# One sample's lookup table, written in front of the scan instead of beside it

## The chip, the cores and the metric

The kernel runs on one core of a Trainium2 chip and processes four images one after the other, with the stages of neighbouring images overlapped. The metric is the device time of one execution, in microseconds. The runs of the kernel before took 21982.39, 21988.68 and 22019.09 us; their median is 21988.68 us.

A core has five engines that work side by side, each through its own instructions in order: PE (TensorE) multiplies matrices, DVE (VectorE) does elementwise work and scans, ACT (ScalarE) does activations and copies, POOL (GpSimd) does elementwise work and issues the indexed gathers, SP (SyncE) issues all other DMAs. They wait for each other through semaphores.

## The reference, cut to what matters

Four layers, each of the form x + f(groupnorm(x)), on images of 128 channels and 128 x 128 pixels in float32:

```python
x = x + _L0_conv_ref(_gn(x), ...)   # deformable 3x3 convolution
x = x + _L1_conv_ref(_gn(x), ...)   # dilated 5x7 convolution and two small products
x = x + _L2_conv_ref(_gn(x), ...)   # projections, a state-space scan in 4 directions, norms
x = x + _L3_conv_ref(_gn(x), ...)   # 3x3 convolution minus a Laplacian
```

Layer 0 is what the change is about. For each pixel and each of 9 taps it samples the normalised image at a position computed from the image, by bilinear interpolation (four corners, four weights, a mask), and multiplies the samples of a tap by a 128 x 128 matrix. Layer 2 holds the heavy part: for each of 4 directions, 128 channels and 16 states a recurrence h = h * exp(delta * A) + delta * u * B over 16384 pixels.

## The kernel before, in words

An image is cut into 32 blocks of 4 rows (512 pixels). Each layer is a Python generator that emits instructions and yields its progress, a number between 0 and 1. A generator's steps are laid out by `weave` (L91): a small software pipeline in which operation `what` of block t minus its lag is emitted at step t. `store` (L133) does not emit a store at once: it puts it on a list, and `tick` (L140) counts it down, three ticks by default, and then emits it on SP.

**The table of layer 0.** `layer0_table` (L236) makes what layer 0 gathers from. It reads the image once for statistics (16 loads of 512 KB, `measure` L251 with 32 bn_stats), computes scale and shift in `gn_affine` (L210), then goes through the 32 blocks: load (256 KB, L270), normalise on ACT (L274), store the normalised block (L275), transpose on PE (four 128 x 128 transposes, L280), copy out of PSUM on ACT (L287), and four stores of 256 KB each (L290), since each entry of the table holds a pixel's four corners side by side. Eight border stores complete it. Its parameter `spare` says whether the transposes go to PSUM bank 2 (`bank(2)`) or to the two buffers `pa` that the scan uses later.

**Layer 0.** `layer0` (L300) works in 288 steps of one block and one tap. A step issues four indirect DMAs on POOL (L426), each fetching 128 table entries of 2 KB; two steps later ACT multiplies three of the corners by their weights (twelve activations, L440), DVE adds and finishes a fourth (L451, L454), PE adds and transposes into one PSUM bank (L464, L465), ACT copies out (`smp`, L469) and PE projects (L475). Every ninth step DVE adds the image (L482). The offsets for the next 16 rows (`positions`, L348) are spread over the same steps. `pw0` sits in bank 2, `pst` in bank 1, `acc` in bank 0, the offsets in bank 3.

**The order around it.** The code at L1352 to L1360 is the part in front of the scan: the first image's table is driven by hand inside the loop over `layer0(sts[0])`, three of its yields per yield of layer 0; then layer 1 of the first image runs alone, then layer 2's first part until four blocks are out. Then `together` (L1313) runs the scan of all four images as the main program, 2048 scan instructions an image (L1044), and beside it one side program. The side program is cut into one part per scanned image by `around` (L1362), and each part is a list of stages with weights that `chain` (L1281) turns into shares of the part. Side work is emitted as the scan goes on, so a stage with weight w in a list with sum W lies beside 2048 w / W scan instructions, whatever its own work is.

Beside the first image's scan the list is: the rest of layer 2's first part of image 0 (18, `begun`), the table of image 1 (12), layer 0 of image 1 (28), layer 1 (14), layer 2's first part (36); the sum is 108. Beside the second and third it is: the end of layer 2 of the image before (16), layer 3 together with the table of the image after next (34), then 28, 14, 36; the sum is 128. `loads` (L1332) marks which engine a stage keeps busy, and the scan moves some of its own work accordingly (with "POOL" some products go to DVE, with "PE" pairs are added on POOL first).

Of the kernel before, what the change touches and what calls it, by code (L numbers as in the profile page):

```python
# [10 lines left out]
F32 = mybir.dt.float32  # L11
# [7 lines left out]
P = 128  # L19
# [4 lines left out]
N = R * W  # L24
# [66 lines left out]
def weave(n, order, ready=lambda t: True):  # L91


    total = n + max(step[0] for group in order for step in group if step is not MORE)
    for t in range(total):
        while not ready(t):
            yield None
        left = iter(())
        for k, group in enumerate(order):
            for step in group:  # L100
                if step is MORE:
                    next(left, None)
                elif 0 <= t - step[0] < n:
                    more = step[1](t - step[0])
                    left = left if more is None else more
            yield (t + (k + 1) / len(order)) / total
        for _ in left:
            pass
# [3 lines left out]
def conv_preact_kernel(ctx: ExitStack, tc: tile.TileContext, a: dict, nb: int):  # L112
# [6 lines left out]
    pss = ctx.enter_context(tc.tile_pool(name="scps", bufs=1, space=PSUM))  # L119
    psb = ctx.enter_context(tc.tile_pool(name="bgps", bufs=1, space=PSUM))  # L120

    def load(pool, src, shape, name, **kw):
        t = pool.tile(shape, F32, name=name, **kw)
        nc.sync.dma_start(t, src)
        return t

    def bank(which, name):
        return psb.tile([P, N], F32, name=name, tag=f"bank{which}")
# [4 lines left out]
    def store(dst, src, after=3, of=None):  # L133

        waiting.append([after, of, dst, src])
# [4 lines left out]
    def tick():  # L140
        for w in waiting:
            w[0] -= 1
        due = [w for w in waiting if w[0] <= 0]
        waiting[:] = [w for w in waiting if w[0] > 0]
        for w in due:
            nc.sync.dma_start(*w[2:])

    def flush():
        while waiting:
            nc.sync.dma_start(*waiting.pop(0)[2:])  # L150
# [45 lines left out]
    def blk(t, i):  # L196
        return t[:, i * N : (i + 1) * N]
# [8 lines left out]
    def rsqrt(dst, src, eps):  # L206
        nc.scalar.activation(dst, src, AF.Ln, bias=eps)
        nc.scalar.activation(dst, dst, AF.Exp, scale=-0.5)

    def gn_affine(stats, which=0):  # L210

        both = bank(which, "pmv")
        mv = small.tile([P, 2], F32, name="mv")
        nc.vector.bn_aggr(mv, stats)
        pm = both[:, 0:1]
        nc.tensor.matmul(pm, gmat, mv[:, 0:1], start=True, stop=True)
        d = small.tile([P, 1], F32, name="gnd")
        nc.vector.tensor_sub(d, mv[:, 0:1], pm)
        e = small.tile([P, 1], F32, name="gne")
        nc.vector.scalar_tensor_tensor(e, d, d, mv[:, 1:2], ALU.mult, ALU.add)  # L220
        pv = both[:, 1:2]
        nc.tensor.matmul(pv, gmat, e, start=True, stop=True)
        sc = small.tile([P, 1], F32, name="gnscale")
        rsqrt(sc, pv, gn_eps)
        sh = small.tile([P, 1], F32, name="gnshift")
        nc.vector.scalar_tensor_tensor(sh, pm, -1.0, sc, ALU.mult, ALU.mult)
        return sc, sh

    def new_stats(b, layer):
        return small.tile([P, NBLK, 6], F32, name=f"stats_{b}_{layer}", tag="stats", bufs=3)  # L230

    def image(name, parts=P):
        return dram.tile([parts, HW], F32, name=name)


    def layer0_table(st, spare=True):  # L236

        xb = x_in[st["b"]].rearrange("c h w -> c (h w)")
        stats = new_stats(st["b"], 0)
        table = dram.tile([TW * TW, 4 * P], F32, name="table")  # L240
        st["rows"] = 0
        tv = table.rearrange("(y x) (q c) -> y x q c", x=TW, q=4)
        xnd = image("xnd")
        with ExitStack() as s:
            lp = s.enter_context(tc.tile_pool(name="l0l", bufs=2, side="right"))
            got = {}

            def fetch(j):
                got[j] = load(lp, xb[:, 2 * j * N : 2 * (j + 1) * N], [P, 2 * N], "xst", bufs=3)

            def measure(j):  # L251
                for i in range(2):
                    nc.vector.bn_stats(stats[:, 2 * j + i, :], blk(got[j], i))

            for f in weave(NBLK // 2, [[(0, fetch)], [(2, measure)]]):
                yield 0.25 * f
            sc, sh = gn_affine(stats, 2)
            st["table"], st["xn"] = table, xnd


            for y, q in ((0, 0), (H, 2)):
                dst = tv[y, :, q : q + 2, :].rearrange("x q c -> x (q c)")
                nc.sync.dma_start(dst[0:W], zero[0:W])
                nc.sync.dma_start(dst[W : W + 1], zero[0:1])
            for x, q, y in ((0, 0, 1), (W, 1, 1), (0, 2, 0), (W, 3, 0)):
                nc.sync.dma_start(tv[y : y + H, x, q, :], zero[:, 0:P])
            yield 0.25

            def fetch_block(i):
                got["x", i] = load(lp, blk(xb, i), [P, N], "xt", bufs=4)  # L270

            def normalise(i):
                got["n", i] = xn = lp.tile([P, N], F32, name="xn", bufs=3)
                nc.scalar.activation(xn, got["x", i], AF.Identity, bias=sh, scale=sc)  # L274
                store(blk(xnd, i), xn)  # L275

            def turn(i):
                got["t", i] = pt = bank(2, "pt") if spare else pss.tile([P, N], F32, name="pt", tag="pa", bufs=2)
                for r in range(R):
                    nc.tensor.transpose(  # L280
                        pt[:, r * P : (r + 1) * P], got["n", i][:, r * W : (r + 1) * W], ident
                    )

            def put(i):
                y = i * R
                gt = lp.tile([P, R, P], F32, name="gt", bufs=4)
                nc.scalar.copy(gt, got["t", i])  # L287
                for q in range(4):
                    ty, tx = y + 1 - q // 2, 1 - q % 2
                    store(  # L290
                        tv[ty : ty + R, tx : tx + W, q, :].rearrange("y x c -> x y c"), gt
                    )
                st["rows"] = i + 1

            for f in weave(NBLK, [[(4, put)], [(0, fetch_block), (2, normalise)], [(3, turn)]]):
                yield 0.25 + 0.75 * f
            flush()
        st["rows"] = NBLK + 1
# [982 lines left out]
    def chain(parts):  # L1281

        total = sum(w for _, w in parts)
        done = 0.0
        for stage, w in parts:
            for f in stage:
                yield None if f is None else (done + w * f) / total
            done += w
# [12 lines left out]
    def rest(stage, when):  # L1301

        first = 0.0
        while not when():
            first = next(stage)
            tick()
        return ((f - first) / (1.0 - first) for f in stage)

    def drain(gen):
        for _ in gen:  # L1310
            tick()
# [17 lines left out]
    sts = [{"b": b} for b in range(nb)]  # L1329
    last = nb - 1  # L1330

    def loads(engine, stage, spare=False):  # L1332
        for f in stage:
            beside["busy"], beside["spare"] = engine, spare
            yield f
        beside["busy"], beside["spare"] = None, False

    def head(b):
        st = sts[b]
        table = [(loads(None, layer0_table(st), True), 12)] if b < 2 else []  # L1340
        return table + [(loads("POOL", layer0(st)), 28), (loads("PE", layer1(st), True), 14),
                (loads("PE", layer2_pre(st), True), 36)]

    def tail(b):
# [5 lines left out]
        return [(post, 16), (loads(load, abreast(conv, layer0_table(sts[b + 2])), True), 34)]  # L1350

    first = head(0)  # L1352
    ahead = layer0_table(sts[0], False)
    for f in layer0(sts[0]):
        tick()
        for _ in range(3):
            next(ahead, None)
            tick()
    drain(chain(first[2:-1]))
    begun = rest(first[-1][0], lambda: sts[0].get("out", 0) >= 4)  # L1360

    def around(b):  # L1362

        side = [(begun, 18)] if b == 0 else tail(b - 1)
        if b < last:
            return side + head(b + 1)
        load, rounds = sum(w for _, w in side), NBLK + 10
        side = [(stage, (NDIR * NBLK + LATE - rounds) * w / load) for stage, w in side]
        return side + [(loads(None, layer2_post(sts[b]), True), rounds)]
# [89 lines left out]
```

## Time and profile before

| what | value |
|---|---|
| median of three runs | 21988.68 us |
| the profiled execution, its time | 22048.69 us |
| its span (first to last instruction) | 22046.9 us |
| mean granted TensorE clock | 0.913 |
| busy share PE, DVE, ACT, POOL | 80, 81, 74, 80% |
| in front of the scan (to its first instruction) | 2328.5 us |
| beside it: scans of image 0, 1, 2, 3 | 5133.9, 5207.0, 5212.5, 3828.7 us |

The profiled execution is 60.0 us longer than the median of the runs; durations below are from it. Inside the part in front of the scan the last block of image 0's table is copied out at 203.4 us, layer 0's gathers run from 220.6 to 1975.7 us, layer 1 follows, and the first scan instruction starts at 2328.5 us. The table of image 1 lies between 3050.8 and 3491.6 us, beside the first scan.

A group's line in the profile reads: line of the code, engine, operation, output and inputs by the program's names, shapes, count, then busy time in us, mean ns of one, and the idle time of the engine just before, with what ended it. A window's line reads: the window in us, its length, each engine's busy time in it with the number of instructions, the granted TensorE clock, the share of the 16 DMA engines in use, and GB/s.

### The profile page before, as it was taken

Reading aid. Unit: us, or ns where it says so; the run is one execution under the profiler, and the core shown is the slowest. Engines: PE = TensorE matmul, PEld = TensorE weight load, DVE = VectorE, ACT = ScalarE, POOL = GpSimd, SP = SyncE. Lnnn points to the kernel's source line nnn. Section 1 sums busy time; section 2 is a strip of 40 time slices with the busy share of each in tenths; the row PEclk is TensorE's granted clock in tenths of the full one; section 3 lists DMA queues with packets and bytes.
Section 4 is the critical chain, followed back from the end, with each engine's and each line's share of the span. In section 5 each row is a group of like instructions: output and inputs, shape, how many; then the busy total and the mean of one; then the engine's idle time right before and its main releaser. Section 6 shows DMA issues by size and latency. Waiting matters only on the chain. (4 is left out here: it accounts for less than half of the span.)

```text
span 22046.9 us, 206313 instructions
## 1 busy us (share of the span) xinstructions
PE 17530.0 (80%) x51536; PEld 8506.2 (39%) x51536; DVE 17759.7 (81%) x18759; ACT 16420.1 (74%) x37439; POOL 17657.2 (80%) x11985
## 2 busy tenths in 40 slices
PE   4667777888878888788888887887887878778788
PEld 3444333445323333454533333344543333233333
DVE  2332688888998899888798889978889888999984
ACT  4775777888778776788868876688877877666673
POOL 3663787667899999777789999977779999999994
PEclk7888998999989999999999999999999999999999
DMA  7666678777766878777776697777776677556674
GB/s 226 189 187 185 191 241 274 245 242 246 255 207 221 237 242 266 243 246 243 246 249 216 219 262 240 257 245 240 250 252 219 221 224 228 200 202 209 214 233 134
DMA packets 2578940, 5040.76 MB, mean 229 GB/s; under 512 B 1060736, under 2 KB 1333576, under 8 KB 2435408
## 3 DMA queue, kind: packets, MB, share of 16 engines
q1 hardware_dynamic: 2209104, 3819.31, 53.2%
q0 software_dynamic: 368640, 1208.25, 18.1%
q8 instruction: 415, 6.80, 0.1%
q14 instruction: 781, 6.40, 0.1%
HBM read 4082.03 MB, written 874.52 MB: 225 GB/s over the span
## 5 line engine op out<-in xcount | busy, mean ns | idle before, releaser
L1044 DVE TENSOR_TENSOR_SCAN h<-pa,carry,h 128x512 f32<-128x512 f32 x8192 | 10011.3, 1267 | 605.7 <-ACT pa L919 386.4
L933 PE MATMUL yacc<-h,gather_sb 128*128 128x512 f32 x15264 | 7958.5, 648 | 1906.5 <-POOL h L959 1303.9
L959 POOL TENSOR_TENSOR h<-h,cb 128x1024 f32<-128x1024 f32 x3651 | 8589.1, 2365 | 622.3 <-ACT carry L953 575.2
L426 POOL DMA_INDIRECT g<-table,idx x4608 | 4535.8, 984 | 2470.2 <-issue 1174.3
L919 ACT ACTIVATE pa<-spread,neg_a 128x512 f32<-128x512 f32 x8192 | 5488.6, 682 | 109.9 <-DVE h L1044 82.3
L933 PEld LDWEIGHTS yacc<-h,gather_sb 128*128 128x128 f32 x15264 | 2967.8, 206 | 6073.5 <-issue 2925.7
L996 DVE TENSOR_TENSOR h<-dub,bb 128x2048 f32<-128x2048 f32 (+1 forms) x2048 | 4210.4, 2056 | 519.8 <-ACT dub L893 517.4
L464 PE MATMUL pst<-ident,g 128*128 128x128 f32 x9216 | 2134.8, 319 | 1327.6 <-ACT smp L469 1097.8
L440 ACT ACTIVATE g<-g,wt 128x128 f32<-128x128 f32 x9216 | 2839.4, 390 | 42.1 <-DMA g<-table,idx 38.9
L953 ACT COPY carry<-h 128x2 f32<-128x2 f32 x4096 | 769.5, 188 | 2705.7 <-DVE h L1044 2699.4
L464 PEld LDWEIGHTS pst<-ident,g 128*128 128x128 f32 x9216 | 1686.8, 224 | 2174.2 <-ACT smp L469 1614.3
L465 PE MATMUL pst<-ident,v 128*128 128x128 f32 x9216 | 2129.5, 318 | 321.9 <-DVE v L454 170.8
L451 DVE TENSOR_TENSOR pw<-pw,g 128x512 f32<-128x512 f32 x1152 | 797.0, 692 | 1961.2 <-ACT pw L440 1555.4
L465 PEld LDWEIGHTS pst<-ident,v 128*128 128x128 f32 x9216 | 1674.8, 227 | 419.2 <-DVE v L454 225.0
L440 ACT ACTIVATE pw<-g,wt 128x128 f32<-128x128 f32 x4608 | 1691.8, 367 | 131.7 <-DVE v L454 11.4
L893 ACT COPY dub<-spread 128x512 f32<-128x512 f32 x2048 | 1195.7, 584 | 302.4 <-DVE h L996 111.8
L454 DVE SCALAR_TENSOR_TENSOR v<-g,wt,pw 128x128 f32<-128x128 f32 x4608 | 1293.6, 343 | 114.4 <-issue 2.3
L475 PE MATMUL acc<-smp,w_sb 128*128 128x512 f32 x2304 | 1287.6, 642 | 21.4 <-DVE x L482 14.8
L469 ACT COPY smp<-pst 128x512 f32<-128x512 f32 x1152 | 668.1, 580 | 776.3 <-remote 578.2
L1264 PE MATMUL p<-xn,w_l_sb 128*128 128x508 f32 (+2 forms) x2304 | 1129.7, 608 | 1.8 <-ACT xn L1243 1.8
L899 POOL TENSOR_TENSOR h<-spread,bb 128x512 f32<-128x512 f32 x845 | 1079.5, 1278 | 15.9 <-DMA spread<-stepsd 10.2
L872 POOL TENSOR_TENSOR e<-e,one_e 128x512 f32<-128x512 f32 x423 | 538.2, 1272 | 486.8 <-ACT one_e L856 463.7
(183 smaller groups left out, 18935.7 us busy)
## 6 DMA issues: line engine op xcount, KB each, us to landing
spread<-stepsd SPq DMA_DIRECT2D x2048, 512.0 KB
bb<-bcd SPq DMA_DIRECT2D x512, 1024.0 KB
cb<-bcd SPq DMA_DIRECT2D x512, 1024.0 KB
stepsd<-steps SPq DMA_DIRECT2D x512, 512.0 KB
table<-gt SPq DMA_DIRECT2D x512, 256.0 KB
g<-table,idx POOLq DMA_INDIRECT x4608
u<-urow SPq DMA_DIRECT2D x256, 256.0 KB
yrow<-y SPq DMA_DIRECT2D x256, 256.0 KB
```

The lines of the kernel that those rows point to most:

```text
L426: nc.gpsimd.indirect_dma_start(out=g[:, r].rearrange("p q c -> p (q c)"), out_offset=None, in_=table, in_offset=bass.IndirectOffsetOnAxis( ...
L440: nc.scalar.activation(pw[:, r * P : (r + 1) * P] if c == 0 else g[:, r, c, :], g[:, r, c, :], AF.Copy, scale=wv[:, r, q, k, c : c + 1],)
L454: nc.vector.scalar_tensor_tensor(v[:, r, :], g[:, r, 3, :], wv[:, r, q, k, 3:4], pw[:, r, :], ALU.mult, ALU.add)
L464: nc.tensor.matmul(dst, g[:, r, 2, :], ident, start=True, stop=False)
L465: nc.tensor.matmul(dst, v[:, r, :], ident, start=False, stop=True)
L475: nc.tensor.matmul(got["a", i], w0[:, k, :], got.pop(("c", n)), start=k == 0, stop=k == KK - 1)
L893: nc.scalar.copy(p, blocks[t]["p", g][:, 1, :])
L919: nc.scalar.activation(pa, blocks[t]["p", g][:, 0, :], AF.Exp, scale=neg_a[:, k, n : n + 1])
L933: nc.tensor.matmul(c["y"], gather[:, g, :], c["h", g][:, ng, :], start=g == 0 and ng == 0, stop=last and ng == parts[-1] and not second,)
L959: engine.tensor_mul(h, h, c["cb"][:, 2 * half : 2 * half + 2, :])
L996: nc.vector.tensor_tensor(h[:, 0:n, :], c["pdu", g].unsqueeze(1).to_broadcast([P, n, N]), c["bb"][:, 0:n, :], ALU.mult)
L1044: nc.vector.tensor_tensor_scan(o, f, o, carry[:, n : n + 1], ALU.mult, ALU.add)
```

## The change

The second image's table is taken off the list beside the first scan and is driven by hand in front of the scan, inside the loop over the first image's layer 0. It starts when layer 0 has passed 0.05 of its progress and is kept level with it from there. It writes its transposes to `pa`, and `gn_affine` takes `pa` too, since bank 2 is in use. `first` has no table entry any more, so layer 1 of image 0 is now its element 1. The countdown of stores changes with it: once the first table is finished, a yield of layer 0 ticks once, and once more for each yield of the second table, where it ticked four times before.

```diff
     def gn_affine(stats, which=0):
-        both = bank(which, "pmv")
+        both = pss.tile([P, N], F32, name="pmv", tag="pa", bufs=2) if which is None else bank(which, "pmv")
...
-            sc, sh = gn_affine(stats, 2)
+            sc, sh = gn_affine(stats, 2 if spare else None)
...
     def head(b):
         st = sts[b]
-        table = [(loads(None, layer0_table(st), True), 12)] if b < 2 else []
-        return table + [(loads("POOL", layer0(st)), 28), (loads("PE", layer1(st), True), 14),
+        return [(loads("POOL", layer0(st)), 28), (loads("PE", layer1(st), True), 14),
                 (loads("PE", layer2_pre(st), True), 36)]
...
     first = head(0)
-    ahead = layer0_table(sts[0], False)
+
+    ahead, second = (layer0_table(st, False) for st in (sts * 2)[:2])
+    at = 0.05
     for f in layer0(sts[0]):
         tick()
         for _ in range(3):
-            next(ahead, None)
+            if next(ahead, None) is not None:
+                tick()
+        while nb > 1 and f is not None and at < f:
+            at = next(second, 1.0)
             tick()
-    drain(chain(first[2:-1]))
+    if nb > 1:
+        drain(second)
+    drain(chain(first[1:-1]))
     begun = rest(first[-1][0], lambda: sts[0].get("out", 0) >= 4)
```

## The prediction

> **What bounds the kernel now.** I read the page's slices first, then the windows of each stage, then the count of scan instructions in the same windows, then the groups of layer 0 in front of the scan. In the slices, columns are busy tenths in 40 equal parts of 551 us.
>
> ```profile
> DVE  2332688888998899888798889978889888999984
> ...
> PEclk7888998999989999999999999999999999999999
> DMA  7666678777766878777776697777776677556674
> ```
>
> The first four parts, in front of the scan, leave DVE at 2 to 3 tenths, the other engines not full either, and PE at a lower clock. From then on DVE is at 8 to 9. The two regimes are limited differently, so I price them apart. The windows below are: layer 0 in front of the scan; beside the first scan `begun`, table, layer 0, layer 1, layer 2's first part; and beside the second scan layer 0, layer 1, layer 2's first part. The limits of a window are where the scan's count passes 2048 times the weight's share.
>
> ```profile
> core 0: us, PE busy (x) PEld busy (x) DVE busy (x) ACT busy (x) POOL busy (x), PEclk, DMA share, GB/s
> 220.60:1975.70 1755.10, 1168.50 (x5662) 840.68 (x5662) 626.54 (x1720) 1229.09 (x3733) 1092.78 (x1152) 0.80 0.64 187
> 2328.50:3050.80 722.30, 605.22 (x1280) 250.80 (x1280) 605.58 (x440) 606.24 (x1128) 638.12 (x364) 0.93 0.68 210
> 3050.80:3491.60 440.80, 297.96 (x640) 118.98 (x640) 407.15 (x323) 292.95 (x583) 368.57 (x199) 0.88 0.93 308
> 3491.60:5613.10 2121.50, 1716.86 (x7270) 1029.07 (x7271) 1797.36 (x2604) 1828.89 (x4990) 1438.51 (x1292) 0.92 0.74 242
> 5613.10:6118.80 505.70, 434.51 (x945) 175.54 (x943) 488.38 (x396) 352.38 (x691) 469.14 (x264) 0.96 0.78 259
> 6118.80:7462.40 1343.60, 1077.23 (x2220) 436.31 (x2220) 1189.19 (x890) 1058.04 (x2014) 1265.14 (x721) 0.92 0.66 215
> 9054.50:11065.20 2010.70, 1629.19 (x7045) 990.76 (x7044) 1598.13 (x2468) 1730.98 (x4795) 1394.10 (x1271) 0.91 0.74 241
> 11065.20:11505.40 440.20, 391.72 (x868) 160.34 (x868) 425.12 (x351) 308.78 (x603) 393.41 (x219) 0.97 0.81 268
> 11505.40:12669.40 1164.00, 960.10 (x1998) 394.75 (x1998) 1011.45 (x756) 940.74 (x1775) 1074.23 (x613) 0.92 0.66 216
> ```
>
> In the table's window DVE is busy 407.15 of 440.80 us: the scan sets the pace there, and the table costs the scan little. Beside layer 0 no engine is over 87%, ACT is first. In front of the scan ACT has 70%, PE 67%, POOL 62%, DVE 36%. The scans of two windows show what a stage carries:
>
> ```profile
> 3050.80:3491.60 440.80, 276.49 (x228) 0.88 0.93 308
> 3491.60:5613.10 2121.50, 671.79 (x533) 0.92 0.74 242
> ```
>
> Layer 0 in front of the scan, 400 to 1800 us:
>
> ```profile
> L426 POOL DMA_INDIRECT g<-table,idx x918 | 870.7, 949 | 528.7 <-ACT smp L469 252.1 <-issue 244.5 <-PE pst L465 25.5
> ...
> L469 ACT COPY smp<-pst 128x512 f32<-128x512 f32 x228 | 133.1, 584 | 391.1 <-remote 350.6 <-PE acc L475 32.3 <-PE pst L465 5.9
> ```
>
> A step takes 6.1 us (1755.1 / 288). ACT idles 391.1 us in this window in front of one instruction, the copy out of `pst`; PE waits in turn for that copy. In the timeline steps of 4.4 us, in which ACT has no gap, alternate with steps of 7.8 us, in which it waits over 3 us. So the loop is a ring PE, ACT, PE with free time in every engine. Last, what a table costs by itself, from 0 to 205 us:
>
> ```profile
> L280 PE MATMUL pt<-ident,xn 128*128 128x128 f32 x128 | 32.5, 403 | 81.4 <-ACT xn L274 81.4
> L274 ACT ACTIVATE xn<-xt,gnshift,gnscale 128x512 f32<-128x512 f32 x32 | 26.0, 813 | 92.4 <-DMA xt<-in_x_dram 92.2 <-DVE gnshift L226 0.2
> L280 PEld LDWEIGHTS pt<-ident,xn 128*128 128x128 f32 x128 | 21.0, 200 | 100.1 <-ACT xn L274 93.2 <-ACT gt L287 3.5 <-issue 3.4
> L253 DVE BATCH_NORM_STATS2 stats<-xst 128x6 f32<-128x512 f32 x32 | 20.4, 684 | 11.0 <-DMA xst<-in_x_dram 10.8
> L287 ACT COPY gt<-pt 128x512 f32<-128x512 f32 x32 | 18.2, 570 | 23.0 <-PE pt L280 21.3 <-DMA table<-gt 1.7
> ```
>
> **What the Trainium skill says.** "Perfetto Trace Analysis", section Optimization Strategy, says that a kernel with several regimes can gain when they are interleaved; the slices show the two regimes, and the change moves work between them. "TensorE: Matmul & The Clock Gate", section What's actually happening, says that the matmul clock is throttled by default and that activity releases it. The trace agrees in direction: 0.80 in layer 0 alone, 0.91 to 0.97 beside a scan. So a few transposes more should not lower it. "DMA: Bandwidth & Descriptors", section Issuing engines are not separate DMA queues, says that DMAs of all engines interleave on the same 16 DMA engines. The trace agrees: between 220 and 1975 us the gathers' queue has 59.3% of them and SP's 4.1%, which is the 0.64 of the window. SP's table traffic will therefore meet the gathers.
>
> **The change, part by part.**
>
> *Removed beside the first scan.* The stage of weight 12 goes: 440.8 us with 2048 x 12/108 = 227.6 scans. The scans do not go. With a sum of 96 instead of 108 they spread over the four stages left: `begun` 341.3 to 384.0 (+42.7), layer 0 531.0 to 597.3 (+66.4), layer 1 265.5 to 298.7 (+33.2), layer 2's first part 682.7 to 768.0 (+85.3). What another scan costs there is read from the same stages beside the second scan, which carry fewer:
> - layer 0: (2121.5 - 2010.7) / (531.0 - 448) = 1.335 us a scan, so +88.6 us
> - layer 1: (505.7 - 440.2) / (265.5 - 224) = 1.58, so +52.4 us
> - layer 2's first part: (1343.6 - 1164.0) / (682.7 - 576) = 1.683, so +143.6 us
> - `begun` has no second window; it is the same work as the stage before, so 1.683, +71.8 us
>
> Sum +356.4 us, net gain 440.8 - 356.4 = 84 us. The gain is the difference between 1.94 us a scan beside the table and 1.57 elsewhere, where scans fill holes. What cuts it: the slope should rise as DVE fills. A bare scan costs DVE 1267 ns (L1044) and a quarter of 2056 ns (L996), 1.781 us; at that price everywhere the scans cost 405 us and the gain is 36 us. At 1.5 throughout it is 99 us. I take the measured slopes. One more wait is in this range: layer 0's buffers now follow directly on layer 2's, on the same side of SBUF, so SP's weight loads wait for the release with the scan's spreads queued behind them; beside the second scan layer 0 also follows a stage on that side, so I add nothing.
>
> *Added in front of the scan.* By instruction:
> - ACT: 32 x (813 + 570) ns = 44 us. In a 4.4 us step this lengthens the ring, in a 7.8 us step it falls into ACT's wait, if it is not queued behind the waiting copy. The copy of the offsets (`pos_c`, L372, 0.6 us, once per strip) shows both: its steps are about 0.5 us longer, and the next two recover about half. Half: 22 us; bounds 0 and 44.
> - PE: 128 transposes, 32.5 us. The nine steps a strip that carry the offsets' convolution (L369, 721 ns each, 432 in the window) take 6.1 us on the mean, like the rest. So a quarter, 8 us; bounds 0 and 33.
> - DVE: 20.4 us of bn_stats beside 64% idle, and one scale-and-shift chain with PE waiting in its middle: 5 us with the last block's tail; bounds 2 and 15.
> - DMA and SP: 216 issues (16 loads of 512 KB, 32 loads, 32 stores and 128 table stores of 256 KB, 8 borders), 59 MB. SP's issue time is some 0.65 us each, 140 us, on a queue that waited 1013.8 us of 400 to 1800 for `x1` (L482). Loads are asked two table steps ahead (some 73 us), the residual for layer 0 over ten of its steps ahead: waiting behind an `x1` store hides. The changed countdown moves stores by three yields, under one step: nothing. In the DMA packets a gather lands 3.65 us after its issue (median), and ACT takes it 4.5 us later (median; 3.1 in the worst twentieth). A block's traffic comes in one burst of four stores, 1 MB, 3.6 us at the 283 GB/s of the first 205 us; delayed by at most that, the gathers are still in time: 1 us in all. Without this cover it is 32 x 2.7 us, as in the second rival.
> - POOL issues nothing new; PSUM `pa` is free until the scan.
>
> Sum 22 + 8 + 5 + 1 = 36 us, with bounds of about 3 and 93 short of the second rival.
>
> *Total.* -84 + 36 = -48 us against the profiled execution's 22048.7, that is 22000.7 for it. The median of the runs is 60.0 us lower: 21988.7 - 48 = 21941 us. Later scans are emitted as before, and nothing is late in place of the table: layer 0 of image 1 starts some 370 us earlier in the first scan, and runs longer.
>
> **The rivals.**
> 1. *No change: the scan is the bound that remains.* The slopes rise to DVE's own 1.78 us, the gain is 36 us and the front costs 36: 21989 us. For it: DVE has 92 to 97% beside table, layer 1 and second layer 1. Against it: beside layer 0 and layer 2 it has 85 to 89%, and two thirds of the moved scans go there, where ACT was busiest.
> 2. *Slower: the bursts break the ring of layer 0.* At each of 32 blocks the stores take half of the DMA engines for 5.4 us (1.5 MB with load and normalised store, at 283 GB/s), the gathers land 2.7 us late after their slack is used up, and ACT and PE pay in full: 32 x 2.7 + 44 + 33 = 163 us, total -84 + 163 = +79, 22068 us. It decides from 84 / 32 = 2.6 us a block. For it: beside the scan, with DMA at 0.74, a twentieth of the gathers land after 6.2 us or more. Against it: the slack above, and 36% of the DMA engines idle.
> 3. *The change does not do what it says.* The emitted order has the table's normalises and copies one block to about seven or eight of layer 0's steps, the last before layer 1's first; so only a wait that stretches it past layer 0 would do this: 21989 us.
>
> **How the numbers follow.** No change means within 0.2%, 44 us, about what a measurement of this kernel can tell. Forecast 0.55 (its own range 21895 to 21975; 0.47 faster, 0.08 within), first rival 0.29 (0.03 faster, 0.24 within, 0.02 slower), second 0.13 (slower), third 0.03 (within). Faster 0.50, within 0.35, slower 0.15. The range 21880 to 22025 has the forecast with the upper gain of 99 us and the low cost, and the first rival with a costlier front; it leaves the second rival out.
>
> **What would show it.** Layer 0 in front of the scan: 1755 becomes about 1791 us, no DMA wait of hundreds of us in front of L440 or L451. First scan: 5134 becomes about 5050 us, its layer 0 about 2210, layer 1 about 558, layer 2's first part about 1487, `begun` about 794. Second and third scan unchanged within 10 us. The forecast is wrong if layer 0 in front grows by over 84 us, or if the first scan shrinks by under 40.

## The result and the profile after

The changed kernel takes 21891.96 us (median of six runs, 21883.9 to 21912.89); the kernel before takes 21988.75 us beside it (six runs). The ratio is 0.9954 with a 95% interval of 0.9943 to 0.9965: 97 us faster where 48 were forecast, inside the range of 21880 to 22025 us, but 3 us beyond the narrower one (21895 to 21975) that the forecast itself was given. A gain of twice the forecast means that terms of the sum were off, so the parts are weighed one by one below.

One caution on the two profiles. The profiled execution of before took 22048.69 us, 60 us more than its runs; that of after took 21889.04, what its runs take. Taken as a pair they would show 160 us. In the later sets of runs the median of the kernel before was 22064, 22077, 22074 and 21533 us. Each of these sets ran on another chip (the record numbers them 15, 7, 13 and 1; the chip of the first set is not given), so absolute times move from set to set by as much as this change is worth or more, and whether the chip does it or something else of a set is open. The stage times that decide are therefore taken from traces whose sets are alike (22064 and 22077 us).

The page's slices of the changed kernel:

```profile
DVE  2332689999988899887798899888888888999984
...
PEclk7888889999899999999999999999999999999999
DMA  8777667777766878777776787777776777556674
```

In front of the scan the DMA engines go from 6 to 7 tenths in most slices, DVE stays at 2 to 3, PE's clock stays at 8. The sixth and seventh slices, where the table lay, fall by one. Two windows carry the result, layer 0 in front of the scan and layer 0 beside the first scan (columns as in the prediction):

```profile
219.00:1960.50 1741.50, 1180.92 (x5792) 852.91 (x5792) 646.33 (x1755) 1265.19 (x3798) 1089.64 (x1152) 0.81 0.73 222
3101.60:5260.40 2158.80, 1760.54 (x7428) 1038.75 (x7428) 1937.01 (x2701) 1902.08 (x5139) 1482.43 (x1308) 0.93 0.77 247
```

Layer 0 in front has 36 us more ACT work than before (1265.19 against 1229.09) and 9 more points of DMA, and is not longer. Layer 0 beside the first scan carries 597 scan instructions instead of 531, with 140 us more DVE work (1937.01 against 1797.36), in 37 us more. Beside the second scan layer 0, layer 1 and layer 2's first part take 2004.5, 440.2 and 1165.9 us, within 7 us of before.

Layer 0 in front, 400 to 1800 us, with the table's groups in it:

```profile
L469 ACT COPY smp<-pst 128x512 f32<-128x512 f32 x231 | 134.5, 582 | 351.8 <-remote 329.8 <-PE acc L475 11.6 <-PE pst L465 5.0
...
L274 ACT ACTIVATE xn<-xt,gnshift,gnscale 128x512 f32<-128x512 f32 x29 | 23.3, 805 | 0.0
...
L287 ACT COPY gt<-pt 128x512 f32<-128x512 f32 x27 | 15.6, 577 | 0.0
```

The table's ACT instructions start with no idle time of ACT before them (0.0 in both lines): they never wait for their data. They take 38.9 us here, and ACT's wait in front of the copy of `pst` falls from 391.1 to 351.8 us: work in exchange for waiting. In the pair of traces from alike sets that is used below (first e_ticks, then after_again), the wait falls from 398.3 to 368.7 us for 38.1 us of work, so some 8 us are not absorbed:

```profile
L469 ACT COPY smp<-pst 128x512 f32<-128x512 f32 x229 | 133.5, 583 | 398.3 <-remote 377.4 <-PE acc L475 17.9
L469 ACT COPY smp<-pst 128x512 f32<-128x512 f32 x227 | 132.5, 584 | 368.7 <-remote 335.0 <-PE acc L475 30.2 <-PE pst L465 1.0
```

### The profile page after: what moved, and what is told of

It reads as the page before. It is cut to its first block, busy times and chain, and to the rows that moved or that the text cites. A ratio compares the mean times of both kernels' runs of the same rounds, so it can differ in the third digit from the quotient of the medians.

```text
span 21887.2 us, 206308 instructions
## 1 busy us (share of the span) xinstructions
PE 17460.2 (80%) x51528; PEld 8474.0 (39%) x51528; DVE 17805.6 (81%) x18780; ACT 16418.2 (75%) x37443; POOL 17610.0 (80%) x11963
```

## The experiments

All were timed against the kernel before; ratios have their 95% interval.

**The table in front, alone (e_front).** The kernel before, its own table kept beside the scan:

```diff
-    ahead = layer0_table(sts[0], False)
+    ahead, extra = layer0_table(sts[0], False), layer0_table(dict(sts[1]), False)
+    at = 0.05
     for f in layer0(sts[0]):
...
+        while f is not None and at < f:
+            at = next(extra, 1.0)
+            tick()
+    drain(extra)
```

> The kernel before, with the second image's table written a second time, in front of the scan beside the first layer 0, into a spare buffer that nothing reads; the list beside the first scan is unchanged (12 for the table, sum 108). It prices the added part alone. The prediction: +36 us (ACT 22, PE 8, the rest 6), so gathers in front take about 1791 us and the whole 22025 us. Rival, free in front: the ring has room, gathers take 1740 to 1760 us, the whole within 15 us of before. Rival, bursts: +160 us, 22150 us.

Measured: ratio 1.0004 (0.9995 to 1.0012), medians 22074.9 against 22064.29 us. A whole extra table, 59 MB with it, costs some 10 us by the medians, and by the interval between nothing and 26 us. Its windows show layer 0 in front and then the table's old place:

```profile
219.30:1984.60 1765.30, 1177.54 (x5792) 852.37 (x5792) 646.24 (x1756) 1264.78 (x3796) 1089.79 (x1152) 0.81 0.72 219
...
3068.10:3508.50 440.40, 296.47 (x640) 119.89 (x640) 407.03 (x324) 292.92 (x583) 368.21 (x199) 0.88 0.93 309
```

Free in front holds, with a remainder of 5 us against 1760.80 in the next kernel, which ran in the same set. The 36 us of the prediction are too much, and the 160 us of the bursts are out.

**The countdown, alone (e_ticks).** The kernel before with `if next(ahead, None) is not None: tick()` in place of the unconditional tick.

> The kernel before with the changed countdown of stores alone: after the first table is finished, a yield of layer 0 ticks once instead of four times, so its stores are emitted some three yields later. Prediction: nothing, within 10 us of before, and gathers in front stay at 1755 us. Rival: the later stores free SP's queue, and the 14 us by which layer 0 in front became shorter (1755.1 to 1741.5 us) come from here: 1741 us.

Measured: ratio 1.0000 (0.9992 to 1.0008), 22065.81 us. It does nothing, so the 14 us by which layer 0 in front got shorter in the first two profiles don't come from it. They are no gain of the table either: the changed kernel has 1741.5 us there in the first set and 1769.0 in a later one. The trace of e_ticks can stand for the kernel before in the comparison of stages. Its windows (layer 0 in front, `begun`, table, layer 0, layer 1, layer 2's first part):

```profile
219.20:1980.00 1760.80, 1168.26 (x5659) 847.98 (x5660) 625.38 (x1719) 1228.01 (x3730) 1089.38 (x1152) 0.80 0.63 186
2333.20:3065.00 731.80, 609.53 (x1280) 252.31 (x1280) 602.58 (x440) 606.08 (x1128) 637.75 (x364) 0.92 0.66 208
3065.00:3508.40 443.40, 292.25 (x640) 116.91 (x640) 407.32 (x323) 292.72 (x583) 368.30 (x199) 0.90 0.92 306
3508.40:5631.70 2123.30, 1706.86 (x7270) 1018.29 (x7271) 1797.01 (x2604) 1827.83 (x4990) 1431.62 (x1292) 0.92 0.74 242
5631.70:6137.20 505.50, 435.18 (x945) 176.05 (x943) 488.24 (x395) 352.36 (x691) 468.76 (x264) 0.96 0.78 259
6137.20:7477.50 1340.30, 1075.40 (x2220) 434.82 (x2220) 1190.17 (x891) 1057.38 (x2014) 1264.47 (x721) 0.92 0.66 215
```

**The place kept, the table gone (e_pad).** The changed kernel with an empty stage in the old place:

```diff
+        pad = [(((i + 1) / 108 for i in range(108)), 12)] if b == 1 else []
-        return [(loads("POOL", layer0(st)), 28), (loads("PE", layer1(st), True), 14),
+        return pad + [(loads("POOL", layer0(st)), 28), (loads("PE", layer1(st), True), 14),
```

> The changed kernel, with an empty stage of weight 12 in the table's old place, which emits nothing: 228 scans run there with nothing beside them, the other stages carry their old number of scans. It separates what the table's work cost beside the scan from what the spreading of its scans over the other stages brings. If the gain is the spreading (the prediction's first step): 228 scans at DVE's 1.78 us take 405 us, 36 us less than with the table, so the whole is some 36 to 50 us under before, and half or more of the gain of 97 us is gone. If the gain is the removal of the table's traffic and work: the stage takes 320 to 350 us and the whole stays within 15 us of the changed kernel, 21890 us.

Measured: ratio 0.999 (0.9982 to 0.9999), 22043.1 against 22064.29 us, 21 us faster. The stage itself:

```profile
3069.00:3480.10 411.10, 286.49 (x508) 105.18 (x508) 387.79 (x287) 257.19 (x515) 367.59 (x199) 0.87 0.57 192
```

228 bare scans take 411.1 us, 32 less than with the table; DMA falls from 0.92 to 0.57 and the time hardly follows, as DVE is still busy 94% of it; 20 of the 32 us are DVE's own work for the table (407.32 against 387.79 us busy). With the 10 us of the front this is the 21 us measured, less than the 36 to 50 expected, which left the front out. The empty stage also does without a third buffer that the scan may use beside the table; DVE idles 4.9 us there for the ACT instruction that fills these buffers, so that matters little. So about a fifth of the gain is the table's own work, and the other four fifths come when its scans are spread over the other stages. Layer 0 in front takes 1767.1 us in this kernel, 6 us more than in e_ticks on the same chip.

**The changed kernel on an equal footing (after_again).**

> The changed kernel once more, unaltered, on the chip of this set: its stage times beside those of the kernel before without a difference between chips. All theories: 0.995 of before; its layer 0 in front takes what it takes in the other kernels of the set, 1755 to 1770 us by the theory that the table is free there, 1741 us by the rival that the table makes layer 0 shorter.

Measured: ratio 0.9954 (0.994 to 0.9967), 21976.17 against 22076.94 us. Its windows, to be held against those of e_ticks:

```profile
219.80:1988.80 1769.00, 1185.42 (x5792) 857.53 (x5792) 646.74 (x1757) 1265.48 (x3796) 1092.74 (x1152) 0.81 0.72 218
2343.70:3139.60 795.90, 650.39 (x1362) 267.33 (x1362) 679.24 (x494) 655.36 (x1224) 715.10 (x407) 0.92 0.67 209
3139.60:5312.50 2172.90, 1751.54 (x7428) 1031.21 (x7428) 1932.35 (x2700) 1901.96 (x5139) 1484.77 (x1308) 0.94 0.76 245
5312.50:5886.70 574.20, 479.83 (x1019) 192.48 (x1018) 550.37 (x445) 391.73 (x773) 528.69 (x296) 0.93 0.76 251
5886.70:7381.80 1495.10, 1179.23 (x2406) 475.39 (x2406) 1339.03 (x995) 1153.29 (x2207) 1418.52 (x805) 0.91 0.65 213
```

| term of the sum | predicted, us | measured, us |
|---|---|---|
| layer 0 in front | +36 | +8 (1769.0 - 1760.8) |
| table's stage gone | -440.8 | -443.4 |
| `begun`, 42.7 scans more | +71.8 | +64.1 |
| layer 0, 66.4 scans more | +88.6 | +49.6 |
| layer 1, 33.2 scans more | +52.4 | +68.7 |
| layer 2's first part, 85.3 scans more | +143.6 | +154.8 |
| sum | -48 | -98 |

Two limits of this table. The ends of the stages are set to whole scan instructions, and at the ends of layer 0 and layer 1 the next scan starts 8 to 10 us later. With every end put on the first scan instruction past the share, the last four rows come to about 63, 57, 52 and 164 us; their sum hardly moves. And the two profiled executions as wholes differ by 72 us, not 98: the second and third scan are 6 and 17 us longer in after_again, though nothing was changed there. The medians of the two kernels differ by 101 us.

**Layer 0's share raised (e_share36).** `(loads("POOL", layer0(st)), 36)` in place of 28 in all three lists.

> The changed kernel with layer 0's weight 36 instead of 28 in all three lists: beside the first scan layer 0 carries 709 scans instead of 597, beside the second and third 542 instead of 448, the other stages fewer. If another scan costs less beside layer 0 than beside the others (1.34 us against 1.58 to 1.68, read from the kernel before): 112 x 0.3 + 2 x 94 x 0.3 = 90 us faster than the changed kernel, 21800 us. If DVE fills up beside layer 0 and the cost rises to its own 1.8 us or more: no change or up to 40 us slower.

Measured: ratio 0.9897 (0.9882 to 0.9912), 21841.69 us: 223 us faster than before, some 120 beyond the changed kernel where 90 were expected. The second and third scan fall to 5147.1 and 5145.5 us (5220.8 and 5231.4 in after_again). The first does not gain: 5046.4 against 5038.2 us, where layer 0 goes from 597 to 709 scans at 1.93 us each. So the slope beside layer 0 is not one number; it is low at 597 and high above.

**Three shares at once (e_three).** Weights 26.55, 41.2 and 43.4 beside the first, second and third scan.

> The changed kernel with three sizes of layer 0's share at once: weights 26.55, 41.2 and 43.4 beside the first, second and third scan, which give layer 0 575, 597 and 620 scan instructions. With 597 (two scan instructions to a step of layer 0) the stage took 2159 us, on the straight line through 448 (2011), 531 (2120) and 709 (2389) it should take about 2216. Theory of an even rhythm: 597 takes 2150 to 2170 us again, 575 and 620 about 2185 and 2250, above the line from their neighbour. Rival, a smooth curve: 2130, 2160, 2200 or 2185, 2216, 2250, without a dip at 597.

Measured: 21913.51 us, ratio 0.9924 (0.9911 to 0.9938). Layer 0's stage, with the scan instructions alone counted (one or two more than the share, as those that cross a window's end count too):

```profile
3143.90:5346.90 2203.00, 724.75 (x576) 0.91 0.74 239
8883.90:11074.60 2190.70, 763.83 (x599) 0.94 0.74 245
14006.00:16286.40 2280.40, 781.03 (x621) 0.92 0.73 238
```

With 575, 597 and 620 scans it takes 2203.0, 2190.7 and 2280.4 us: 22 scans more cost less than nothing, the next 22 cost 90 us. The value at 597 lies 20 us above the expected interval, still under its neighbour with fewer scans. The three stand beside different scans, but the dip is there in one place too: beside the first scan 597 take 2172.9 us in after_again of the same set, 30 less than 575 here, and beside the third 597 take 2188.2 us in e_even below, 92 less than 620 here. So the smooth curves are out. Counted over the gathers alone (first to last of a layer's 1152, scan instructions begun in between), from the traces of five kernels:

| scan instructions per step of layer 0 | gathers take, us |
|---|---|
| 1.50 | 1936 to 1944 |
| 1.77 | 2025 |
| 1.81 | 2028, 2038 |
| 1.92 | 2098 |
| 1.99 | 2067, 2069 |
| 2.00 | 2094, 2099, 2102 |
| 2.07 | 2188 |
| 2.38 | 2287 |

With just under or at two scan instructions to a step the time is that of 1.92, or up to 30 us less; past two it jumps by some 90 us. The values at 1.92 and 2.07 are from one trace each. The changed kernel has 574 in 288 steps, 1.99. The name given to this, an even rhythm, is a reading: no view shows why the step is short there.

**PE kept active (e_warm4, e_warm8).** Behind each projection of layer 0 in front, four or eight times:

```diff
+                for _ in range(warm):
+                    nc.tensor.matmul(idle[:, 0:P], ident, ident, start=True, stop=True)
```

> The changed kernel with four matmuls of 128x128 more in each step of layer 0 in front of the scan, behind the projection, into a PSUM tile that nothing reads; they only keep PE active. If the granted clock of 0.80 holds the step at 6.1 us and activity raises it: clock above 0.9, steps near POOL's 5.04 us (4 gathers of 1.26 us), gathers 1450 to 1600 us, the whole 150 to 290 us faster than the changed kernel. Rival, PE is in the ring with its busy time: 4 x 0.27 us a step, up to 310 us slower.

> The same with eight matmuls more a step. If activity raises the clock and four are too few: the gain shows here. Rival: PE's busy time counts, up to 620 us slower than the changed kernel; if four already lose, this loses twice as much.

Measured: 22001.36 and 22040.99 us, ratios 0.9968 (0.9955 to 0.9981) and 0.9984 (0.9977 to 0.9991), so about 25 and 65 us slower than the changed kernel. The window 400 to 1800 us of the one with eight:

```profile
400.00:1800.00 1400.00, 1209.73 (x8021) 991.84 (x8020) 502.95 (x1372) 973.27 (x2918) 833.60 (x879) 0.93 0.70 212
```

The granted clock goes from 0.81 to 0.93, and fewer gathers fit (879 against 911 in after_again). More activity does raise the clock, and raising it in this way buys nothing. PE's work doesn't count in full either: 8 x 288 more matmuls, 287 ns each by the trace, are 661 us, and the gathers take 60 us more. But the two effects stand against each other here. The products of the turn went from 345 and 337 ns to 297 and 294, by an estimate from these means 0.7 us for the sixteen of a step, while eight matmuls of 287 ns, 2.3 us, were put in PE's order in front of the next turn. So this does not show that the clock has no part in the step's length.

**Two PSUM banks for the turn (e_twobank), the even shares (e_even), both (e_both).** In front, every other `pst` goes to a second bank; beside the second and third scan layer 0's weight is 41.2 instead of 28:

```diff
-                got["t", n] = pst = bank(1, "pst")
+                odd = front and n % 2
+                got["t", n] = pst = pss.tile([P, N], F32, name="pst", tag="yacc") if odd else bank(1, "pst")
...
-        return [(loads("POOL", layer0(st)), 28), (loads("PE", layer1(st), True), 14),
+        return [(loads("POOL", layer0(st)), 28 if b < 2 else 41.2), (loads("PE", layer1(st), True), 14),
```

> The changed kernel with layer 0's weight 41.2 beside the second and third scan, 28 beside the first: layer 0 then carries 597 scan instructions in all three, two to a step. By the theory of an even rhythm each of the two scans takes 5133 us, as the second did with 598 in the kernel of three sizes, instead of 5220 to 5231: about 180 us faster than the changed kernel, some 21795 us where that takes 21976. Rival, the good second scan there was chance: 60 to 120 us faster, as with 542 scans beside layer 0 (5146 us a scan) or less.

> The changed kernel with layer 0 in front of the scan turning into two PSUM banks by turns instead of one, so that PE need not wait for ACT's copy of the step before. If that one bank is what holds the step at 6.1 us, the wait of PE for the copy goes and a step comes to POOL's 5.04 us: gathers about 1460 us, the whole up to 300 us faster than the changed kernel. If the step is held elsewhere (the gathers on POOL, the four buffers of gathered data, the order on ACT): gathers 1700 to 1770 us, within 70 us of the changed kernel.

> Both together, the even shares and the two banks: their gains lie in different parts of the time and should add to within 20 us.

Measured: even shares 21801.4 us, ratio 0.9879 (0.9864 to 0.9894); two banks 21958.5, 0.9949 (0.9936 to 0.9963); both 21786.34, 0.987 (0.9855 to 0.9885). The even shares come out as forecast from e_three, before they ran: the second and third scan take 5135.4 and 5129.1 us, layer 0 in them 2181.3 and 2188.2 us with 150 scans more than the 2012.9 and 2018.7 with 448 in e_twobank of the same set, 1.13 us a scan, under what the same scans cost elsewhere. The two banks are worth little: 15 us on top of the even shares in the same set, and against the changed kernel, which ran in another set, less than the intervals can tell. Layer 0's gathers in front take 1759 us with them, PE's wait for the copy falls, and in its place PE waits for DVE and the copy for PE. One bank alone is not what holds the step. The two gains add, as was expected. The kernel with both beats the two kernels of this case, by 1.3% against before.

**More buffers for gathered data (e_deep).** `bufs=6` instead of 4 for `g` in front.

> The changed kernel with six buffers instead of four for the gathered data of layer 0 in front of the scan; nothing else. If POOL's waits for a free buffer hold the step at 6.1 us, the gathers run ahead, POOL's waits for the copy out of PSUM go (287.6 us of 400 to 1800), and gathers take 1460 to 1650 us, the whole 100 to 300 us faster than the changed kernel. If the order on ACT and PE holds it and POOL merely follows: gathers 1740 to 1770 us, no change.

Measured: 21449.23 against 21532.99 us, ratio 0.9961 (0.9946 to 0.9975). This set is the one in which the kernel before is 456 to 544 us faster than in the others. Layer 0 in front took 1441 us there, POOL's pace (5.00 us a step), and ACT's wait for `pst` is gone:

```profile
L469 ACT COPY smp<-pst 128x512 f32<-128x512 f32 x256 | 147.9, 578 | 5.0 <-PE pst L465 4.6
```

The trace alone would give this to the buffers. The ratio does not: had they brought the 300 us, it would be about 0.981, and it is the changed kernel's own 0.9954 within the interval. So the kernel before should have had the shorter front in this set too, and the buffers show no gain that can be told. A second sum says the same: e_deep's trace is 555 us shorter than that of after_again, 327 of it in layer 0 in front and 228 in stages whose buffers were not touched. Had the 327 been the buffers', the kernel before would be some 228 us faster in this set than in that one, and it is 544. No trace of a kernel with four buffers was taken there, so how much of the 1441 us is the set's and how much the buffers' is argued from these sums, not shown.

## Why the prediction was right, and where its sizes were wrong

The time came out inside the range, and both halves of the mechanism are seen: the table is nearly free in front (e_front), and what is gained beside the scan is above all the spreading of 228 scan instructions over other stages (e_pad). Where that gain comes from was only half right, and in part it was luck.

*Removed stage*: right to 3 us (440.8 against 443.4).

*Added in front*: mis-sized, 36 us for 5 to 8. The prediction charged 22 us of ACT's 44, taking half of the steps to be without a gap, and 8 us on PE. The stage grew by 8 us, in e_front by 5 and in e_pad by 6. Steps without a gap alternate with steps in which ACT waits over 3 us, and ACT's wait shrank by most of the work added, so a delay in one step seems to be taken out of the wait of a later one. The probe that was used, the copy of the offsets, showed that recovery for two steps only, and it was charged as if it stopped there. Nothing speaks against the price of 1 us for DMA: gathers land later in the changed kernel (each gather paired in order with its packets, the worst twentieth 5.6 us after issue instead of 4.1), and ACT still takes them a median of 4.4 us after landing, in the worst tenth 2.7 us.

*Spread scans*: 356 us predicted, 337 measured, from two errors of opposite sign. Layer 0's 88.6 us were 50 to 57: the straight slope of 1.335 us from 448 and 531 scans does not hold at 597. Layer 1 and layer 2's first part, where DVE or POOL is already over 90%, cost 20 to 28 us more than the slopes said: together 1.8 to 1.9 us a scan, as the first rival had it. Layer 1 alone can't be told, since its slope, the predicted one too, hangs on where its ends are put (52 or 69 us). Against bare scans at 1.81 us (411.1 us for 227.6), layer 0 saves about 63 to 70 us, `begun` 13, and the two others nothing. The holes that the prediction saw in four stages were thus found in two.

*Luck*: 597 scans happen to lie at two to a step of layer 0, which nobody had looked at. With 575 layer 0 takes 2203.0 us beside the first scan (e_three), 80 us more than with 531 in e_ticks, 1.8 us a scan, as much as a bare one. A share that missed the dip could have left much less of the gain.

*The rest*: the first scan came to 5038 us against 5144 in e_ticks, 106 us less where 84 were predicted. In the traces of the other kernels that leave the second and third scan as they were (e_deep, on the fast chip, aside), these scans take 5199 to 5220 and 5202 to 5229 us, so the 6 and 17 us in the pair can't be told from that scatter. The first rival fails as a whole: it charged the front 36 us, and its 1.78 us a scan held only beside layer 1 and layer 2's first part. The second rival needed 2.6 us a block; e_front has 5 to 10 us over 32 blocks, at most 0.3 us. The third is out: the table's copies end in front of the scan, at 1955.6 us. One reading of the trace was short: beside a scan the granted clock is 0.88 to 0.97, not 0.91 to 0.97, since the table's own window has 0.88.

What is left open: what holds layer 0's step in front at 6.1 us where POOL's issues need 5.04. It is not the one PSUM bank alone (e_twobank); the buffers are excluded only by the sums of e_deep, and the clock is not excluded. The ring PE, ACT, PE, in which the prediction saw the cause, is shown in one half only: PE waits for the copy, but what the copy waits for is not seen. Of the 391.1 us that ACT waits for the copy in before, 350.6 are put down to "remote", a release that the profile names no instruction for. Two lines of its timeline:

```profile
1007.71 0.39 PE L465 MATMUL pst<-ident,v 128*128 128x128 f32 x2
1012.61 0.59 ACT L469 COPY smp<-pst 128x512 f32<-128x512 f32 x1 [3.31 <-remote]
```

By the record the last product that the copy needs ends 4.5 us before it, and ACT is idle for 3.3 of them. All 89 waits of over 2 us between 400 and 1600 us are of this kind, with a median of 4.4 us from the product's end to the copy; the trace of e_deep has no wait over 2 us there.

## What to carry to other kernels

When side work is handed out by weights, taking one stage away is priced by what the main work costs in each stage that inherits it, not by the stage's own length; those slopes can be read from places where the same stage carries different amounts. A slope between two points need not hold beyond them: here the time dipped where two iterations of one loop met one of the other, so look at that ratio before extrapolating, and try a share on either side. A loop whose engine waits in front of one instruction can take in other work at little cost: here 38 us went into 398 us of waits, and the loop grew by 8. How near to the full size of the waits this goes was not tried.

## What was not expected of the hardware

The same kernel before had medians from 21533 to 22077 us in five sets, a spread of 2.5%; four of the five are known to be from different chips. The one trace of the fastest set has ACT waiting 5.0 us for the copy out of PSUM between 400 and 1800 us, against 352 to 398 us in the traces of the other sets. That trace is of the kernel with six buffers, so it is argued and not shown that a large part of the spread between sets lies in how this one loop runs. And a granted clock raised from 0.81 to 0.93 by idle matmuls went with a longer loop, not a shorter one, though with the idle matmuls themselves in it.
